# The thin last column block of A in two graph products: one fetch into one buffer in place of two fetches into two

## The chip, the cores and the metric

The kernel runs on one core of a Trainium2 chip. The metric is the device time of that core in microseconds (us); 904 us is about the time of one execution. An execution is one launch of the whole four-layer network. "PE" is the matrix engine, "DVE" the vector engine, "ACT" the scalar (activation) engine, "POOL" the general engine, "SP" the engine that here only issues transfers; "SPq" is its queue.

## The reference, cut to what matters

Four graph layers run one after the other on N = 2708 nodes with F = 128 features. `A` (`adj` in the code) is a dense stored 2708 x 2708 float32 matrix, 29.3 MB. Each layer ends in `x = layernorm(x + layer(x))`.

```python
# layer 0: x = LN(x + (D^-1/2 (A+I) D^-1/2 @ x) @ W.T + b)
# layer 1, attention:
XW  = x @ W
den = exp(leaky_relu(s_row[:, None] + s_col[None, :]))
num = A @ den
att = where(num != 0, den / num, 0)
H   = A @ (att @ XW)                 # product "a1" of the kernel
x   = LN(x + H)
# layer 2, hyperbolic:
xt  = logmap0(proj(mobius_add(proj(mobius_matvec(W2, x)), bias)))
s   = A @ xt                         # product "a2"
x   = LN(x + proj(expmap0(relu(logmap0(proj(expmap0(s)))))))
# layer 3:
out = concat((A > 0) @ x, (A < 0) @ x) @ Wn + bn * diag(A) + (A @ x) @ We + be * diag(A) + x
x   = LN(x + out)                    # products "a3": A and the mask of A
```

## The kernel before, in words

Features lie on the 128 partitions and nodes run along the free axis, so a product with A is computed transposed, from the stored `adjT`. The contraction over nodes is cut into NT = 22 row tiles of 128 (the last has 20 rows), and the result into NB = 6 column blocks: five of BW = 512 columns and a last one of 148. One block of one product is 22 accumulating matmuls of 128 x 128 against 128 x 512 (or 128 x 148) float32. A float32 matmul shows as two matmul passes in the trace, so a block has 44 passes and a whole product 264.

The stage before (the attention) ends at about 474 us. After it the function `fast_rest` runs the products a1, a2 and a3 one behind the other, and streams A from DRAM once for each. `pieces(b, i)` fetches half a column block: 11 row tiles of block `b` (KH = 11), with `i` the half. The second half has ten full row tiles by one transfer and the 20-row tile by another. A wide half is 2,816 KB or 2,560 + 40 KB; a half of the thin block is 814 KB or 740 + 11.6 KB. Each call takes the next of three buffers in turn: two in the pool `cb_a` and one in `cb_b`, by `n % 3`, where `n` counts the calls. All three have the shape of a wide half. A buffer is free again when the last matmul (in a3 also the last mask) that reads the piece in it is done. All the transfers stand in SP's queue in the order of the calls, and SP waits at each one for its buffer. In the kernel before, a1 takes pieces 0 to 11, a2 takes 12 to 23 and a3 takes 24 to 35. I call them by these numbers where needed, or by product, block and half: "a2 block 0, first half".

`product(weights, b, name, upto)` issues the matmuls of one block, up to row tile `upto`, and asks for a piece when it reaches the first tile of a half. `after_attention(b)` works on a finished block of a1: residual, layer norm, and the first product of layer 2 (`mx`). `hyperbolic(q, ta, tb)` does the scalar work of layer 2 on groups of row tiles, (0, 12) after block 2, (12, 20) after block 4 and (20, 22) after block 5, in long chains of tiny vector instructions with square roots, logarithms and tanh on ACT between; it ends by writing `h` (`q_b` in the trace), the weights of a2, one row tile after the other (line 1717). `meanwhile` puts the first six matmuls of a2's block 0, two at a time, between the steps of block 5 of `after_attention`, with a hand-written order on PE.

`after_hyperbolic(b)` works on a finished block of a2: sums (`su`), a mean that is spread back (`mean`), a factor that is spread back (`pg`), a norm (`st`, `pr_l`), and the products `pp` that make `edge` and `node`, the weights of a3. In a3 each row tile takes one float32 matmul from the piece itself (line 1867) and two one-pass matmuls (line 1876) against a mask of the piece that DVE makes (line 1855), in tiles of at most six row tiles; two such mask tiles exist.

Two seams matter in what follows: the one from a1 to a2, and the one from a2 to a3. At each of them the thin block 5 of one product is followed by the wide block 0 of the next. Apart from the hand-written stretch, a scheduler sets the order of the instructions on each engine from its own expectation of when the operands are ready[...].

Of the kernel before, what the change touches and what calls it, by code (L numbers as in the profile page):

```python
# [10 lines left out]
F32 = mybir.dt.float32  # L11
# [10 lines left out]
P = 128  # L22
NT = (N + P - 1) // P
NP = NT * P
BW = 512
NB = (N + BW - 1) // BW
KH = NT // 2
# [17 lines left out]
def rows(t):  # L45
    return min(P, N - t * P)


def width(b):
    return min(BW, N - b * BW)  # L50
# [7 lines left out]
def kernel(  # L58
# [130 lines left out]
    @contextmanager  # L189
    def queued(*engines):  # L190

        traced = nc.cur_bb.bb.instructions
        n = len(traced)
        with ExitStack() as st:
            for e in engines:
                if e in latest:
                    st.enter_context(tc.issue_after(latest[e]))
            yield
        for i in traced[n:]:
            if i.engine in engines:  # L200
                latest[i.engine] = i
# [5 lines left out]
    def bslice(b):  # L207
        return slice(b * BW, b * BW + width(b))
# [632 lines left out]
    with tc.tile_pool(name="tri", bufs=1) as tp:  # L841
# [241 lines left out]
        for c in range(NB):  # L1083
            w = width(c)
# [83 lines left out]
    with ctx_keep:  # L1168
# [11 lines left out]
        with tc.tile_pool(name="sort", bufs=1) as st_p:  # L1180
# [45 lines left out]
            for b in range(NB):  # L1226
                w, cs = width(b), bslice(b)
# [174 lines left out]
    def grouped_attention(u_sb, rows_g):  # L1402
        adj_h = adjT.rearrange("k (h w) -> (k h) w", h=2)
        chunks = [(0, BW), (BW, 2 * BW), (2 * BW, HALF)]
        with tc.tile_pool(name="main", bufs=1) as mp:
# [146 lines left out]
            for t in range(HALF // P, NT):  # L1552
                node_major_u(t, t % 2)

    def fast_rest(u_sb, pieces, scratch_pool, blk):


# [17 lines left out]
        def product(weights, b, name, upto=NT, fixed=False):  # L1575


            w = width(b)
            if name not in begun:
                begun[name] = [psum.tile([P, BW], F32, tag=f"acc{3 + b % 3}", name=name), 0, None]  # L1580
            acc, done, pc = begun[name]
            for k in range(done, upto):
                i, t = divmod(k, KH)
                if t == 0:
                    pc = pieces(b, i)
                kw = rows(k)
                with queued(PE) if fixed else nullcontext():
                    nc.tensor.matmul(  # L1588
                        acc[:, :w],
                        lhsT=weights[:kw, k, :],  # L1590
                        rhs=pc[:kw, t, :w],
                        start=(k == 0),
                        stop=(k == NT - 1),
                    )
            begun[name] = [acc, upto, pc]
            return acc

        def meanwhile(b, n):

            if b == NB - 1:  # L1600
                product(h, 0, "a2_0", n, True)
                return queued(PE)
            return nullcontext()
# [178 lines left out]
        for b in range(NB):  # L1782
            after_attention(b, product(u_sb, b, f"a1_{b}"))
            if b in spans:
                hyperbolic(b, *spans[b])
# [53 lines left out]
        for b in range(NB):  # L1839
            after_hyperbolic(b, product(h, b, f"a2_{b}"))  # L1840
# [5 lines left out]
        for b in range(NB):  # L1846
            w, cs = width(b), bslice(b)
            acc = psum.tile([P, BW], F32, tag=f"acc{3 + b % 3}", name=f"a3_{b}")
            for i in range(2):
                pc = pieces(b, i, i == 1)  # L1850
                for ma, mb in ((0, 6), (6, KH)):
                    mask = scratch_pool.tile([P, 6, BW], F32R, tag="mask", name=f"mask{b}_{i}_{ma}", bufs=2)
# [10 lines left out]
                    for t in range(ma, mb):  # L1863
                        k = i * KH + t
# [28 lines left out]
    with tc.tile_pool(name="cb_b", bufs=1) as cb_b, tc.tile_pool(name="cb_a", bufs=2) as cb_a:  # L1893
        u_sb = xw
        rows_g = cb_b.tile([P, KH, BW], F32, tag="cb", name="rows_g").rearrange("p t c -> p (t c)")
        grouped_attention(u_sb, rows_g)
        with (
            tc.tile_pool(name="rest", bufs=1) as rest_p,
            tc.tile_pool(name="blk2", bufs=2) as blk2,
        ):  # L1900
            pools["blk"] = blk2
            count = {"n": 0}

            def pieces(b, i, diagonal=False):

                n = count["n"]
                count["n"] += 1
                pool = cb_b if n % 3 == 2 else cb_a
                t = pool.tile([P, KH, BW], F32, tag="cb", name=f"cb{n}")
                w, cs = width(b), bslice(b)  # L1910
                full = KH - i
                k0 = i * KH * P
                if n < 3:

                    with tc.issue_after(marks["begun"]):
                        nc.gpsimd.memset(t[:, :, 0:1], 0.0)
                nc.sync.dma_start(
                    out=t[:, :full, :w],
                    in_=adjT[k0 : k0 + full * P, cs].rearrange("(t p) c -> p t c", p=P),
                )  # L1920
                if i:
                    kw = rows(NT - 1)
                    nc.sync.dma_start(out=t[:kw, full, :w], in_=adjT[k0 + full * P :, cs])
                    if diagonal:
                        nc.sync.dma_start(
                            out=t[kw : kw + 1, full, :w], in_=diag_d[cs, :].rearrange("c o -> o c")
                        )
                return t

            fast_rest(u_sb, pieces, rest_p, blk2)  # L1930
# [47 lines left out]
```

## Time and profile before

Three runs took 903.33, 903.94 and 903.99 us.

| what | value |
|---|---|
| median of the runs | 903.94 us |
| the profiled execution: its span | 903.4 us |
| PE busy | 847.1 us, 94% of the span |
| DVE / ACT / POOL busy | 554.8 / 389.0 / 206.1 us |
| mean granted PE clock | 0.973 of full speed |
| HBM read | 179.33 MB, 203 GB/s over the span |
| first and last matmul of a1 | 474.1 and 586.6 us |
| first and last matmul of a2 | 589.7 and 717.1 us |
| first and last matmul of line 1867 (a3) | 720.8 and 894.1 us |
| the chain that ended last | 84% PE, 8% DMA, 5% DVE, 2% ACT |

In the profile's lists of work in order of time, a line gives the start and the length in us, the engine, the source line, the operation with its operands and shape, and the count of the instructions merged into it. A bracket says how long the engine had sat idle before the line, and what ended the wait. The granted clock tells what share of its full rate the matrix engine was given in a stretch.

### The profile page before, as it was taken

What the parts mean: (1) busy time and instruction counts of PE and PEld (TensorE: products, weight loads), DVE (VectorE), ACT (ScalarE), POOL (GpSimd) and SP (SyncE); (2) the same over time, 40 slices, a digit from 0 to 9 for tenths busy, and PEclk for the clock granted to TensorE, in tenths of its full rate; (3) what the DMA queues carried; (4) which work ended last, traced back from release to release, by engine and by line L of the source; (5) the groups of instructions that cost most, each with busy time, mean ns of one, the idle gap of its engine ahead of it and who ended that gap; (6) DMA issues with size and microseconds to landing.
All of it is one profiled execution on the core that took longest, in us unless ns stands there. A gap on an engine that the chain in (4) does not pass through costs nothing.

```text
span 903.4 us, 9470 instructions
## 1 busy us (share of the span) xinstructions
PE 847.1 (94%) x3268; PEld 429.5 (48%) x3268; DVE 554.8 (61%) x1189; ACT 389.0 (43%) x681; POOL 206.1 (23%) x176
## 2 busy tenths in 40 slices
PE   3699999699899999999999999989999899999996
PEld 3244454335344445444454444534444555555555
DVE  4777548988788888889971226375644564233313
ACT  3776433215787777787761115273332221000000
POOL 5221000101788885776500000000000000000000
PEclk9799999989899999999999999999999999999997
DMA  9995684596596555445534776496764565474410
GB/s 341 366 361 204 120 245 144 182 383 215 180 372 213 151 162 158 142 153 154 154 122 168 266 268 229 134 335 238 265 222 132 210 211 198 145 253 142 160 42 19
DMA packets 95979, 184.30 MB, mean 204 GB/s; under 512 B 6446, under 2 KB 23551, under 8 KB 95668
## 3 DMA queue, kind: packets, MB, share of 16 engines
q1 hardware_dynamic: 85700, 143.82, 46.2%
q0 software_dynamic: 8352, 37.76, 13.0%
q10 hardware_dynamic: 1872, 2.04, 0.7%
q8 instruction: 28, 0.46, 0.2%
q14 instruction: 27, 0.22, 0.1%
HBM read 179.33 MB, written 4.28 MB: 203 GB/s over the span
## 4 chain that ended last, share of the span: by engine, by line
PE 84%; DMA 8%; DVE 5%; ACT 2%; issue 1%; SPq 0%; DVEq 0%; ACTq 0%
PE a L1588 22%; PE num L1464 13%; PE uacc L1491 13%; PE a L1867 12%; PE a L866 10%; PE a L1876 6%; DMA A<-in_adjT_dram 4%; DMA B<-in_adjT_dram 3%; PE t L803 1%; DMA cb<-in_adjT_dram 1%; PE pp L1825 1%; DVE counts L1051 1%; PE mx L1695 1%; PE su L251 0%; DVE work L267 0%
## 5 line engine op out<-in xcount | busy, mean ns | idle before, releaser
L1415 POOL DMA_INDIRECT rows_g<-in_adjT_dram,row_i x52 | 131.2, 2523 | 90.6 <-PE num L1464 40.9
L1469 ACT ACTIVATE ln<-num,inval,occ_l 128x512 f32<-128x512 f32 x156 | 107.5, 725 | 52.7 <-DVE rows_g L1467 48.7
L1867 PE MATMUL a<-cb,ut 128*128 128x512 f32 (+2 forms) x264 | 125.8, 559 | 1.3 <-DMA cb<-in_adjT_dram 1.3
L1491 PE MATMUL uacc<-att,xw_g 128*128 128x512 f32 (+1 forms) x312 | 126.3, 542 | 0.0
L1876 PE MATMUL a<-mask,node 128*128 128x512 f32 (+2 forms) x264 | 120.3, 537 | 0.7 <-DVE mask L1855 0.7
L1464 PE MATMUL num<-rows_g,w_all 128*128 128x512 f32 (+1 forms) x276 | 113.6, 544 | 0.8 <-ACT ln L1469 0.8
L1588 PE MATMUL a<-cb,q_b 128*128 128x512 f32 (+2 forms) x264 | 111.7, 561 | 1.8 <-DMA cb<-in_adjT_dram 1.8
L866 PE MATMUL a<-A,q_b 128*128 128x512 f32 (+2 forms) x264 | 106.1, 549 | 1.5 <-DMA A<-in_adjT_dram 1.5
L1588 PE MATMUL a<-cb,xw 128*128 128x512 f32 (+2 forms) x264 | 107.3, 550 | 0.0
L1467 DVE COPY rows_g<-num 2x512 f32<-2x512 f32 x150 | 88.0, 612 | 15.8 <-PE num L1464 14.6
L1491 PEld LDWEIGHTS uacc<-att,xw_g 128*128 128x128 f32 x312 | 59.1, 190 | 59.1 <-issue 50.0
L1483 DVE TENSOR_TENSOR att<-att,ln 128x1354 f32<-128x1354 f32 x52 | 80.5, 1548 | 2.0 <-ACT ln L1479 2.0
L1464 PEld LDWEIGHTS num<-rows_g,w_all 128*128 128x128 f32 x276 | 49.8, 190 | 53.8 <-issue 39.6
L1876 PEld LDWEIGHTS a<-mask,node 128*128 128x128 f32 (+1 forms) x264 | 48.5, 193 | 49.4 <-issue 47.6
L230 ACT ACTIVATE sq_l<-s 128x512 f32<-128x512 f32 (+1 forms) x11 | 6.6, 604 | 148.4 <-DVE s L1885 116.7
L1479 ACT ACTIVATE ln<-ln 128x1354 f32<-128x1354 f32 x52 | 69.3, 1333 | 1.7
L1855 DVE TENSOR_SCALAR mask<-cb 128x3072 fp32r<-128x3072 f32 (+5 forms) x24 | 33.5, 1395 | 59.3 <-PE a L1876 58.6
L866 PEld LDWEIGHTS a<-A,q_b 128*128 128x128 f32 (+1 forms) x264 | 45.9, 191 | 50.0 <-issue 46.7
L1588 PEld LDWEIGHTS a<-cb,q_b 128*128 128x128 f32 (+1 forms) x264 | 45.1, 192 | 46.9 <-issue 42.8
L1588 PEld LDWEIGHTS a<-cb,xw 128*128 128x128 f32 (+1 forms) x264 | 45.1, 190 | 46.5 <-issue 46.5
L1074 ACT ACTIVATE xw<-A 128x2048 f32<-128x2048 f32 (+3 forms) x36 | 57.0, 1582 | 8.3 <-DMA b_s<-in_b_dram 4.4
L1456 DVE TENSOR_SCALAR att<-q_b,gj_l 128x1354 f32<-128x1354 f32 x52 | 48.2, 927 | 12.6 <-PE uacc L1491 12.5
(445 smaller groups left out, 899.5 us busy)
## 6 DMA issues: line engine op xcount, KB each, us to landing
cb<-in_adjT_dram SPq DMA_DIRECT2D x15, 2816.0 KB
cb<-in_adjT_dram SPq DMA_DIRECT2D x15, 2560.0 KB
A<-in_adjT_dram SPq DMA_DIRECT2D x25, 1024.0 KB
B<-in_adjT_dram SPq DMA_DIRECT2D x18, 1024.0 KB
cb<-in_adjT_dram SPq DMA_DIRECT2D x3, 814.0 KB
cb<-in_adjT_dram SPq DMA_DIRECT2D x3, 740.0 KB
ut<-in_adjT_dram SPq DMA_DIRECT2D x2, 1024.0 KB
A<-in_adjT_dram SPq DMA_DIRECT2D x5, 296.0 KB
```

The costliest lines, as they stand in the source:

```text
L866: nc.tensor.matmul(acc[c][:, :w], lhsT=z[:kw, k, :], rhs=t[:kw, i, :w], start=c not in begun, stop=(d == NB - 1 and k == NT - 1), skip_gro ...
L1074: checks[d, c] = nc.scalar.activation(below[:, :nt, :w], t[:, :nt, :w], AF.Relu, scale=-1.0, accum_out=neg_sum[:, NB * c + d : NB * c + d ...
L1415: got = nc.gpsimd.indirect_dma_start(out=gat[q], out_offset=None, in_=adj_h, in_offset=bass.IndirectOffsetOnAxis(ap=row_i[:, h, g : g + 1] ...
L1464: nc.tensor.matmul(num[:, : cb - ca], lhsT=w, rhs=gat[q][:, ca:cb], start=True, stop=True)
L1467: nc.vector.tensor_copy(gat[q + 1][0:2, ca:cb], num[0:2, : cb - ca])
L1469: nc.scalar.activation(ln_n[q][:, ca:cb], num[:, : cb - ca], AF.Ln, scale=occ_l[:, g : g + 1], bias=inval[:, g : g + 1],)
L1479: nc.scalar.activation(ln_n[q], ln_n[q], AF.Exp, scale=-1.0)
L1483: nc.vector.tensor_mul(att[q], att[q], ln_n[q])
L1491: nc.tensor.matmul(uacc[h][c][:, : cb - ca], lhsT=xw_g[:, g, :], rhs=att[q][:, ca:cb], start=(g == 0), stop=(g == GM - 1),)
L1588: nc.tensor.matmul(acc[:, :w], lhsT=weights[:kw, k, :], rhs=pc[:kw, t, :w], start=(k == 0), stop=(k == NT - 1),)
L1867: nc.tensor.matmul(acc[:, :w], lhsT=edge[:ke, k, :], rhs=pc[:ke, t, :w], start=(k == 0), stop=False, skip_group_check=True,)
L1876: nc.tensor.matmul(acc[:, :w], lhsT=node[:kw, k, j, :], rhs=mask[:kw, t - ma, :w], start=False, stop=(k == NT - 1 and j == 1), skip_group_ ...
```

## The change

`product` asks for the thin block (b = 5) as one piece of all 22 row tiles, and `pieces` gives it one buffer of the tile's real width, 22 x 148 elements a partition, 13,024 bytes, where a wide half is 11 x 512, 22,528 bytes. The 21 full row tiles come by one transfer of 1,554 KB and the 20-row tile by a second of 11.6 KB. This holds for a1 and a2. a3 still asks for two halves of its thin block. With it the calls of `pieces` are numbered anew: a1 takes pieces 0 to 10, a2 takes 11 to 21 and a3 takes 22 to 33; the rule `n % 3` is unchanged.

```diff
             acc, done, pc = begun[name]
+            half = NT if b == NB - 1 else KH
             for k in range(done, upto):
-                i, t = divmod(k, KH)
+                i, t = divmod(k, half)
                 if t == 0:
-                    pc = pieces(b, i)
+                    pc = pieces(b, i, n_full=half)
...
-            def pieces(b, i, diagonal=False):
+            def pieces(b, i, diagonal=False, n_full=KH):
...
                 pool = cb_b if n % 3 == 2 else cb_a
-                t = pool.tile([P, KH, BW], F32, tag="cb", name=f"cb{n}")
                 w, cs = width(b), bslice(b)
-                full = KH - i
+                cols = BW if n_full == KH else w
+                t = pool.tile([P, n_full, cols], F32, tag="cb", name=f"cb{n}")
+                ends = i == 1 or n_full == NT
+                full = n_full - ends
                 k0 = i * KH * P
...
-                if i:
+                if ends:
                     kw = rows(NT - 1)
                     nc.sync.dma_start(out=t[:kw, full, :w], in_=adjT[k0 + full * P :, cs])
```

## The prediction

> **What bounds the kernel now.** I read the shares of busy time first: PE is busy 94% of the span, so only stretches in which PE is idle, or runs slowly, can give time back. In the groups of instructions, the two float32 groups of the last three products that wait at all wait for a fetch of A:
>
> ```profile
> L1867 PE MATMUL a<-cb,ut 128*128 128x512 f32 (+2 forms) x264 | 125.8, 559 | 1.3 <-DMA cb<-in_adjT_dram 1.3
> L1588 PE MATMUL a<-cb,q_b 128*128 128x512 f32 (+2 forms) x264 | 111.7, 561 | 1.8 <-DMA cb<-in_adjT_dram 1.8
> ```
>
> By that view the stake is 3.1 us. It is more, as PE's work in order of time shows at the seam from a1 to a2:
>
> ```profile
> 586.77 1.16 PE L1695 MATMUL mx<-w2ext,x 128*128 128x129 f32 x8
> 589.69 1.98 PE L1588 MATMUL a<-cb,q_b 128*128 128x512 f32 x4 [1.76 <-DMA cb<-in_adjT_dram]
> 591.51 0.50 PE L1612 MATMUL st<-mean_w,asq 128*128 128x1 f32 x4
> 591.88 1.96 PE L1588 MATMUL a<-cb,q_b 128*128 128x512 f32 x4
> 596.17 0.66 PE L244 MATMUL pr<-ident,rstd 128*128 128x128 f32 x2 [2.33 <-DVE t L1717]
> 596.62 3.29 PE L1588 MATMUL a<-cb,q_b 128*128 128x512 f32 x4
> 599.75 0.61 PE L1695 MATMUL mx<-w2ext,x 128*128 128x129 f32 x4
> ```
>
> See the bracket of the second line (the piece is late), the bracket before `pr` (a vector result is late), and that four passes take 3.29 us where four took 1.96. The same view at the seam from a2 to a3:
>
> ```profile
> 714.74 2.68 PE L1588 MATMUL a<-cb,q_b 128*128 128x148 f32 x18
> 719.05 0.40 PE L273 MATMUL pg<-two_pg,sel 128*128 128x128 bf16 x4 [1.64 <-DVE two_pg L267]
> 720.75 1.13 PE L1867 MATMUL a<-cb,ut 128*128 128x512 f32 x2 [1.30 <-DMA cb<-in_adjT_dram]
> 722.55 1.22 PE L1876 MATMUL a<-mask,node 128*128 128x512 f32 x2 [0.67 <-DVE mask L1855]
> 723.57 1.91 PE L1867 MATMUL a<-cb,ut 128*128 128x512 f32 x2
> ```
>
> Busy time and granted clock by stretches of 1 us tell the rest. Columns: stretch, length, busy time with counts of PE, PEld, DVE, ACT and POOL, the granted clock, the DMA share, GB/s.
>
> ```profile
> 597.00:598.00 1.00, 1.00 (x2) 0.34 (x1) 0.69 (x5) 0.43 (x2) 0.00 (x0) 0.50 1.05 389
> 600.00:601.00 1.00, 1.00 (x6) 0.57 (x5) 0.93 (x8) 0.58 (x2) 0.00 (x0) 1.00 1.05 383
> 724.00:725.00 1.00, 1.00 (x2) 0.00 (x0) 0.71 (x2) 0.98 (x2) 0.00 (x0) 0.50 1.06 391
> ```
>
> After each group of pauses the clock is halved, here for about 3.4 us. The issue queue says why the pieces are late. A row merges neighbours: the first is the issue at 558.54 and one that ends at 570.63.
>
> ```profile
> 558.54 12.09 SPq L1917 DMA_DIRECT2D cb<-in_adjT_dram  x2
> 579.89 4.11 SPq L1917 DMA_DIRECT2D cb<-in_adjT_dram  x2
> 587.51 17.53 SPq L1917 DMA_DIRECT2D cb<-in_adjT_dram  x2
> 697.39 0.58 SPq L1923 DMA_DIRECT2D cb<-in_adjT_dram  x1
> 709.58 4.99 SPq L1917 DMA_DIRECT2D cb<-in_adjT_dram  x2
> ```
>
> The thin halves hold two of three buffers, so a2's first half (piece 12) is issued at 579.89 and a3's (piece 24) at 709.58, some 8 us before PE needs them. Piece 24 is released to PE 11.1 us after issue, while the next pieces share the engines (385 to 412 GB/s).
>
> [...]here SP waits 187.7 us in all for matmuls of line 1588 ahead of line 1917.
>
> **The change part by part.** Sums are against the span of 903.4 us; the median is 903.94, 0.5 us above it, and I carry the difference over.
>
> *Buffers.* With the thin block in one buffer, a2's first half takes the buffer that block 4's first half leaves at 570.6, not 579.9. The nearest undisturbed estimate of its landing: DMA moves about 390 GB/s when full, 2,816 KB is 2.88 MB, 7.4 us;[...] 9.6 us. It lands at 580.2; PE needs it at 587.9. The second half follows at 579.9 (lands about 588.7) and block 1's first half still at 587.5 (about 596). At the other seam a3's first half is issued where 697.4 was, 12.2 us earlier relative to PE's work. Both fetch waits, 1.76 and 1.30 us, go, with 8 us of cover.
>
> *The thin fetch.* It is issued where its first half was (558.5) and needed at 581.9. The halves, in 592-byte runs, each kept the engines busy for 3 to 4 us; 1,554 KB is then 6 to 8 us[...]. It lands by 569, hidden by 12 us of block 4. In a2 the spare is the same. One issue fewer (0.37 us of SP) lies in SP's waiting: nothing.
>
> *The order at the first seam.* The built programs' orders differ. PE's is the same up to a2's row tile 11. On ACT the root of block 5's variance (line 1685) moves up, directly behind block 4's root, and needs no table load of its own (1.28 us before). On DVE its reciprocal (1686) moves from behind block 4's chain to its start. So after `mx` at 587.93: four passes to 589.7, `st` to 590.1, root to 590.5, reciprocal to 590.9, while PE works to 591.9. The 2.33 us wait goes. With both pauses gone the slow clock goes: from 596.17 to 600.19 PE did what takes 0.22 + 1.75 + 0.44 = 2.4 us at full clock, so 1.6 us. First seam: 1.76 + 2.33 + 1.6 = 5.7 us.
>
> *What is late next.* Row tiles 12 to 19 of `h` come from the chain of block 4. In the new order 22 instructions of block 5 stand among it, ahead of its last factor. Bounds: nothing, if they fall in the 0.2 us steps of the dependent chain, or 22 x 0.2 = 4.4 us. Eight of them pair with eight dependent steps and are free; 14 at 0.1 us, less some gaps, are about 1.1. Row tile 12 was written at 601.86 to 602.2; I take 603.3. PE's new order puts row tiles 6 to 11 and three matmuls of block 1 before it: 594.5 + 9 x 0.875 = 602.4. New wait 0.9 us; at the upper bound 4.2, and then a slow clock of 1.6 again. Row tiles 20 and 21 were ready at 616.5; their chain starts 5.7 us earlier and waits behind two table loads, so about 612.7 to 613, against PE at about 613.8: no wait.
>
> *The second seam.* PE now reaches a3's block 0 with its piece landed. DVE's first two masks (1.76 and 1.48 us) move ahead of block 4's sums, and ten of a3's matmuls (four float32, six mask) ahead of `pg`: 4 x 0.88 + 6 x 0.23 = 4.9 us of work. The masks push block 4's chain about 1.3 us, to `two_pg` at 720 where it was 719.0, in before's times; PE asks at 722.3. So 1.64, 1.30 and 0.67 us all go. From 722.55 to 726.47 PE did what takes 0.46 + 0.86 + 0.36 + 0.57 = 2.25 us: 1.6 us of slow clock. Together 5.2 us. Given back: DVE's third mask now stands before block 4's norm, waits for PE's sixth row tile, and takes 1.76; then 2.15 us to `two_pr_l`; PE has three row tiles, 4.0 us, to cover 3.9 plus hand-over. I take 0.3 us for this and the `pp` behind it; bounds 0 and 2.2, the cover less one row tile and the mask's wait doubled.
>
> Sum: 5.7 + 5.2 - 0.9 - 0.3 = 9.7 us. After the seams PE waited for nothing until the last norm, so a gain made here reaches the end. Span 893.7, median 894.2.
>
> **The rivals.**
> A: *the hyperbolic chain takes the place of the fetch.* For it: h's rows were only 3 us ahead of PE, and the chain gets 22 insertions. Against: most fit in gaps, and block 5's part starts earlier. If the upper bound holds, the first seam gives 5.7 - 5.8, nothing: 903.94 - 4.9 = 899.0.
> B: *the vector queue blocks at the second seam*: third mask, norm and `pp` each late, with a slow clock again. For it: the 0.1 us margin above. Against: each stall is short. It leaves the first seam's 4.8: 899.1.
> C: *no change.* Both A and B, or the pieces don't move: 903 to 904. Against: SP's queue is limited by nothing but the buffers.
> D: *slower.* The masks now stand ahead of block 4's sums[...]. If a3's first half lands late, because one thin fetch drains slowly ahead of it, every us beyond some 2.4 of cover stops DVE, then PE. It was to land in 9.6 us; to eat 9.7 us as well it must be 12 us late, so take 22 us. Just beyond, at 24 us: 906. The measured rates speak against it; a loss by something I don't see goes here too.
>
> **How the numbers follow.** Forecast 70%, A 12%, B 6%, C 5%, D 7%. The forecast's own range is 893 (no new wait: 903.94 - 10.9) to 897. I give 892.6 to 899.2, which takes in A and B and leaves out C and D. Differences under 0.2% (1.8 us) can't be told from none. Faster 0.70 + 0.12 + 0.06 = 0.88, same 0.05, slower 0.07.
>
> **What would show it.** No fetch bracket at lines 1588 and 1867 of the seams; no bracket at `pr` near 590 to 592; `pg` without a wait; the clock at 1.00 through both seams; a2's end at 717.1 less about 4.8. A bracket by DVE's line 1717 at a2's row tiles 12 to 20 over 1 us, or a second slow stretch, shows A; one at `pr_l` or `pp`, B. I am wrong if a fetch is still late, or if time goes in a stage that the change doesn't touch.

## The result, and the profile after

| | runs | median, us | lowest to highest |
|---|---|---|---|
| before, beside it | 4 | 903.63 | 899.73 to 903.99 |
| changed | 4 | 893.93 | 892.15 to 894.80 |

The ratio is 0.9895, with an interval of 0.9876 to 0.9913: faster by 9.7 us. A later set of five runs gave 893.42 and a ratio of 0.9889 (0.9868 to 0.9909).

The profiled execution of the changed kernel has a span of 890.3 us, 13.1 less than that of before. That is more than the runs gained, so I split it by stage, from PE's work in order of time. Each number is the start of a product's last matmul with A:

| | first of a1 | last of a1 | last of a2 | last of a3 (the float32 ones) |
|---|---|---|---|---|
| before | 474.1 | 586.6 | 717.1 | 894.1 |
| changed | 472.7 | 585.2 | 710.0 | 881.1 |

a1 starts 1.4 us earlier; over all profiled executions of this study it starts anywhere from 471.5 to 477.6, whatever the kernel. That is scatter of the stages before it, which the change doesn't touch. a1 itself takes 112.5 us in both. From a1's end to a2's end, the stretch with the first seam, it is 130.6 and 124.8, so 5.8 us gained; from a2's end to a3's end, with the second seam, 176.9 and 171.1, so 5.8 (taken before rounding to 0.1). These two stretches carry the rest of the document, since the scatter of a1's start is not in them.

The groups of instructions of the changed kernel, at the two groups that waited for a fetch before (busy us and mean ns of one, then the idle time ahead; the lines have moved by one):

```profile
L1868 PE MATMUL a<-cb,ut 128*128 128x512 f32 (+2 forms) x264 | 123.6, 550 | 0.0
L1589 PE MATMUL a<-cb,q_b 128*128 128x512 f32 (+2 forms) x264 | 110.4, 555 | 0.1
```

The idle time has gone from 1.3 and 1.8 us to 0.0 and 0.1. The mean matmul is shorter too (559 to 550 ns, 561 to 555): the stretches at half clock are gone. PE's work in order of time at the first seam:

```profile
585.38 1.16 PE L1696 MATMUL mx<-w2ext,x 128*128 128x129 f32 x8
586.38 1.88 PE L1589 MATMUL a<-cb,q_b 128*128 128x512 f32 x4
...
590.26 0.38 PE L244 MATMUL pr<-ident,rstd 128*128 128x128 f32 x2
590.48 1.88 PE L1589 MATMUL a<-cb,q_b 128*128 128x512 f32 x4
```

and at the second:

```profile
708.85 1.42 PE L1589 MATMUL a<-cb,q_b 128*128 128x148 f32 x8
710.19 1.13 PE L1868 MATMUL a<-cb,ut 128*128 128x512 f32 x2
...
715.14 0.39 PE L273 MATMUL pg<-two_pg,sel 128*128 128x128 bf16 x4
...
723.24 0.40 PE L273 MATMUL pr_l<-two_pr_l,sel 128*128 128x128 bf16 x4
```

No line has a bracket, which these lists put only at idle times over 0.15 us. Where `mx` ends, a2's first matmul begins, and where a2 ends, a3's first begins. The four passes behind `pr` take 1.88 us, where they took 3.29. The clock by stretches, at the places that were at 0.50 before or close behind them:

```profile
597.00:598.00 1.00, 1.00 (x4) 0.51 (x3) 1.00 (x13) 0.68 (x3) 0.00 (x0) 1.00 0.00 0
724.00:725.00 1.00, 1.00 (x5) 0.53 (x4) 0.36 (x1) 0.00 (x0) 0.00 (x0) 1.00 0.00 0
```

The clock, third from the end, is 1.00. The last two, DMA share and GB/s, are nothing: the fetch that ran at about 390 GB/s here in before is already over. SP's queue shows why:

```profile
557.15 0.37 SPq L1920 DMA_DIRECT2D cb<-in_adjT_dram  x1
...
568.87 10.00 SPq L1920 DMA_DIRECT2D cb<-in_adjT_dram  x2
...
689.82 12.97 SPq L1920 DMA_DIRECT2D cb<-in_adjT_dram  x2
```

557.15 is the thin block of a1 in one transfer. The issue at 568.87 is a2's first half (its second half closes the row, at 578.87), 17.5 us before PE uses it at 586.38; before, it was issued 9.8 us ahead. At 689.82 a3's first half is issued, 20.4 us before its use.

### The profile page after: what moved, and what is told of

The parts are those of the page before. It is cut to its first block, busy times and chain, and to the rows that moved or that the text cites. A ratio compares the mean times of both kernels' runs of the same rounds, so it can differ in the third digit from the quotient of the medians.

```text
span 890.3 us, 9463 instructions
## 1 busy us (share of the span) xinstructions
PE 840.4 (94%) x3268; PEld 425.4 (48%) x3268; DVE 552.1 (62%) x1189; ACT 386.2 (43%) x679; POOL 205.3 (23%) x176
## 4 chain that ended last, share of the span: by engine, by line
PE 85%; DMA 7%; DVE 5%; ACT 2%; issue 1%; SPq 0%; DVEq 0%; ACTq 0%
PE a L1589 22%; PE num L1464 13%; PE uacc L1491 13%; PE a L1868 11%; PE a L866 10%; PE a L1877 6%; DMA A<-in_adjT_dram 4%; DMA B<-in_adjT_dram 3%; PE t L803 1%; PE pp L1826 1%; DVE counts L1051 1%; PE su L251 1%; PE mx L1696 1%; DVE work L267 0%; PE st_l L251 0%
## 5 line engine op out<-in xcount | busy, mean ns | idle before, releaser
L1868 PE MATMUL a<-cb,ut 128*128 128x512 f32 (+2 forms) x264 | 123.6, 550 | 0.0
```

What stands on the lines that cost most here:

```text
L1868: nc.tensor.matmul(acc[:, :w], lhsT=edge[:ke, k, :], rhs=pc[:ke, t, :w], start=(k == 0), stop=False, skip_group_check=True,)
```

## The experiments

All numbers of a stretch are from the profiled execution of that kernel. "First seam" is the stretch from a1's end to a2's end, "second seam" from a2's end to a3's end.

| kernel | median, us | ratio to before, interval | first seam | second seam |
|---|---|---|---|---|
| before | 903.6 to 904.3 | | 130.6 | 176.9 |
| changed | 893.93 | 0.9895 (0.9876 to 0.9913) | 124.8 | 171.1 |
| again | 893.42 | 0.9889 (0.9868 to 0.9909) | 124.8 | 171.7 |
| only_a1 | 899.09 | 0.9951 (0.9932 to 0.9969) | 124.8 | 175.7 |
| only_a2 | 897.26 | 0.9934 (0.9914 to 0.9955) | 128.9 | 171.1 |
| two_buffers | 903.68 | 1.0003 (0.9986 to 1.0020) | 130.5 | 176.7 |
| two_transfers | 894.97 | 0.9906 (0.9881 to 0.9931) | 124.8 | 171.1 |
| root_early | 905.28 | 1.0012 (0.9999 to 1.0025) | 130.1 | 176.9 |
| root_late | 899.44 | 0.9953 (0.9929 to 0.9977) | 130.8 | 171.2 |
| filled | 902.92 | 0.9993 (0.9981 to 1.0004) | 128.9 | 176.8 |

**again.** The changed kernel once more.

> The changed kernel once more, for a tight figure against the kernel before on the same chip. Both seams together gained 5.8 and 5.9 us in the profiled executions (11.7 in all), while the medians differ by 9.7. If the seams are the whole of it, the difference of the medians here is 10 to 12 us and the rest of the 9.7 was scatter between runs; if some of the 11.7 is given back elsewhere, it stays below 10.

The ratio held, and the medians differ by 10.6 us, inside the 10 to 12 expected if the seams are the whole of it. The second seam was 171.7 instead of 171.1: in this execution the thin last block of a3 ran 3.4 us at half clock, as it did in before, and in the profile of the changed kernel it did not. Up to the start of that thin block the second seam is 163.68 us in before, and 158.45 and 158.44 in the two executions of the change. So 5.2 of the 5.8 us belong to the change, and 0.6 is a clock that happened to stay up. It is only 0.6 because at full clock PE then waits 0.89 us for `pr_l` in that block (at 873.20); at half clock, in `again`, that wait doesn't occur.

**only_a1, only_a2.** The thin block in one buffer in one product only.

```diff
-            half = NT if b == NB - 1 else KH
+            half = NT if b == NB - 1 and name[:2] == "a1" else KH
```

The other one has "a2" there.

> The thin block as one piece in a1 alone. If the two seams are independent, it gains the first seam's 5.7 us (5 to 6.5), and the trace shows the pauses and the half clock of before still at the seam from a2 to a3. Rival: the gain hangs on both changes (a start of a2 that is earlier is only waited off at the next seam), then it gains under 2 us.

> The thin block as one piece in a2 alone. Independent seams: it gains the second seam's 5 to 6.5 us, with the first seam as before (1.76 us of fetch wait, 2.3 us before pr, half clock). With the run of a1 alone it adds up to the whole change within 1 us. Rival as there: under 2 us.

The stretches come apart as the theory has it: only_a1 has the whole gain of the first seam (124.8), only_a2 the whole gain of the second (171.1). The ratios multiply to 0.9885, against 0.9889 for the whole. The medians are looser: 5.0 and 6.8 us under before, where 5 to 6.5 was expected of each, and 11.7 together against 10.6 for `again`. Each kernel also has a little in the seam that its edit leaves alone. In only_a1 it is 1.2 us: the third pause of the second seam, 0.67 us for a mask, didn't occur (the clock was at 0.50 earlier there, from 715.63 to 719.04, and a3's first two passes took 1.83 us where before took 1.13), and the thin last block stayed at full clock (0.6). In only_a2 it is 1.6 us, and PE's work in order of time shows how:

```profile
587.30 3.51 PE L1589 MATMUL a<-cb,q_b 128*128 128x512 f32 x4 [1.94 <-DMA cb<-in_adjT_dram]
...
593.59 0.40 PE L244 MATMUL pr<-ident,rstd 128*128 128x128 f32 x2 [0.61 <-DVE t L1718]
```

The clock was at 0.50 right behind the first pause, from 587.00 to 590.41, so four passes took 3.51 us there; PE came to `pr` that much later, and waited 0.61 us for the root instead of 2.33. A slow clock ahead of a wait cost nothing here; behind the last wait, as in before, it cost about 1.6 us.

**two_buffers, two_transfers.** Which part of "one piece" counts, the buffer or the transfer? In two_buffers the 21 full row tiles come as in the change, in one transfer of 1,554 KB, but the 20-row tile goes to the next buffer in turn, so that two buffers are held as before. In two_transfers there is one buffer, and the 21 row tiles come in two transfers, as the halves did. In two_buffers

```diff
+                end = t
+                if n_full == NT:
+                    n = count["n"]
+                    count["n"] += 1
+                    pool = cb_b if n % 3 == 2 else cb_a
+                    end = pool.tile([P, n_full, cols], F32, tag="cb", name=f"cb{n}")
...
-                    nc.sync.dma_start(out=t[:kw, full, :w], in_=adjT[k0 + full * P :, cs])
+                    nc.sync.dma_start(out=end[:kw, full, :w], in_=adjT[k0 + full * P :, cs])
```

and in two_transfers

```diff
+                cuts = (0, KH, full) if n_full == NT else (0, full)
+                for ca, cb in zip(cuts, cuts[1:]):
+                    nc.sync.dma_start(
+                        out=t[:, ca:cb, :w],
+                        in_=adjT[k0 + ca * P : k0 + cb * P, cs].rearrange("(t p) c -> p t c", p=P),
+                    )
```

> The thin block by one transfer for its 21 full row tiles, as in the change, but the 20-row tile goes into the next buffer, so that the block again holds two of the three until its last matmul. Theory (the buffer is what matters): a2's and a3's first halves are issued as late as before, both fetch waits and both slow clocks are back, and the time is that of the kernel before within 1.5 us. Rival (the one large transfer, its fewer issues, is what matters): the time is that of the changed kernel, about 10 us faster.

> The change, with the 21 full row tiles of the thin block fetched by two transfers (11 and 10 row tiles) into the one buffer. Theory: same as the changed kernel within 1 us (about 10 us under the kernel before), since the buffers are the same and the issue costs 0.4 us of SP's waiting. Rival (the single transfer matters): slower than the changed kernel by over 2 us.

With two buffers held, nothing is left of the gain (1.0003), and both pauses of the first seam stand as they did:

```profile
587.62 1.98 PE L1589 MATMUL a<-cb,q_b 128*128 128x512 f32 x4 [1.72 <-DMA cb<-in_adjT_dram]
...
594.13 0.66 PE L244 MATMUL pr<-ident,rstd 128*128 128x128 f32 x2 [2.36 <-DVE t L1718]
```

With one buffer and two transfers all of it is there (0.9906, stretches equal to the change's). It is the buffer. How the bytes are cut makes no difference that these runs can tell.

**root_early, root_late.** In the first seam the change does two things: the piece comes early, and the scheduler moves the root of block 5's variance ahead of block 4's chain. root_early is before, with its late piece, but with the new place of the root: block 4's hyperbolic group is issued behind block 5's part of `after_attention`, and its first logarithm is held behind block 5's reciprocal. root_late is the change, with its early piece, but with block 5's root held behind block 4's tanh, as it was.

Root_early, against before:

```diff
+            marks["root"] = nc.vector.reciprocal(rstd[:, ta:tb], rstd[:, ta:tb]).ins
...
+            with tc.issue_after(marks["root"]):
+                arg = atanh(f"a{q}", z, n)
...
-            if b in spans:
+            if b == 2:
...
+        for b in (4, 5):
+            hyperbolic(b, *spans[b])
```

Root_late, against the change:

```diff
+            with tc.issue_after(marks["tanh"]) if b == NB - 1 else nullcontext():
+                nc.scalar.activation(rstd[:, ta:tb], st[:, :n], AF.Sqrt, bias=eps_c)
...
+            marks["tanh"] = nc.scalar.activation(rn, arg, AF.Tanh).ins
```

> The kernel before, with its two pieces in two buffers, but block 5's root of the variance on ACT and its reciprocal on DVE ahead of block 4's logarithm, as the changed kernel has them. Theory: the fetch is still late (1.76 us), the 2.33 us before pr go, but block 4's chain now waits for the late root by about 2 us, and PE at a2's row tile 12 waits for it 2 us: 901 to 903 in all, against 904.0 of before. Rival (at the first seam the order alone brings the gain, not the fetch): 898 to 899.5, as with the change in a1 alone.

> The changed kernel, but with block 5's root held behind block 4's tanh on ACT, as the kernel before had it. The fetches are as early as in the change. Theory: no fetch bracket, but PE stands before pr for about 4.5 us, and the clock halves after it (1.6 us): it loses 5 to 6.5 us against the changed kernel, so about 899. Rival (the early fetch alone is the gain of the first seam): within 2 us of the changed kernel.

Neither half brings more than 0.5 us in the first seam: 130.1 and 130.8 against 130.6, where both together give 124.8. With the root early and the piece late, `pr` doesn't wait any more, but block 4's chain now waits for block 5's reciprocal, that for the sum `st`, and that for PE, which stands at the late piece. The list of PE's waits, in the stretch from 585 to 640 us of root_early (total, times, longest), has what was saved at `pr` back at a2's later row tiles:

```profile
PE a L1588 <- DVE q_b L1717: 2.9, 2, 2.7
```

That made root_early a miss of my expectation on the slow side. With the piece early and the root late, PE gets to `pr` sooner and waits there for all of it:

```profile
595.45 0.40 PE L244 MATMUL pr<-ident,rstd 128*128 128x128 f32 x2 [4.36 <-DVE t L1719]
```

4.36 us is more than the two pauses of before together (1.76 + 2.33). The two waits were in a row; taking away one of them feeds the other. At the second seam the early piece and the new order were not taken apart in this way: only_a2 brings both, two_buffers takes both away.

**filled.** What is the half clock worth? Before, with added matmuls at PE's two pauses in the first seam, so that the engine works while it waits.

```diff
+        def fill(ps, n):
+            for _ in range(n):
+                nc.tensor.matmul(ps, lhsT=ident, rhs=x[:, :BW], start=True, stop=True)
...
+                    fill(st, 1)
...
+                    fill(pr, 2)
```

> The kernel before with three added matmuls (128x512 float32, into a scratch tile that is overwritten) in the first seam: one ahead of a2's first matmul, where the engine waits 1.76 us for the piece, two ahead of `pr`, where it waits 2.33 us. Buffers, fetches and the orders of DVE and ACT are those of before, so the piece and the root still come late, but the matrix engine is kept at work while it waits. The pauses should shrink to less than 1.2 us in all. Theory (the pauses halve the clock, and that costs about 1.6 us): no half clock in the first seam, a1's end to a2's end 128.9 where before has 130.5, second seam as in before, whole time about 902.4. Rival (what the half clock costs is taken from a wait that would be there anyway, or it is set by something else than the pauses): 130.5 and about 903.9.

PE's work in order of time, where the first and third lines are the added matmuls:

```profile
587.47 1.02 PE L1607 MATMUL st<-x,ident 128*128 128x512 f32 x2
589.48 1.98 PE L1588 MATMUL a<-cb,q_b 128*128 128x512 f32 x4 [0.98 <-DMA cb<-in_adjT_dram]
...
593.46 1.88 PE L1607 MATMUL pr<-x,ident 128*128 128x512 f32 x4
595.76 0.43 PE L244 MATMUL pr<-ident,rstd 128*128 128x128 f32 x2 [0.42 <-DVE t L1726]
```

The pauses shrank to 0.98 and 0.42 us, the clock stayed at 1.00 through the first seam, and the stretch is 128.9, or 1.7 us less: what the half clock cost here, about the 1.6 expected, can be had alone, by useless work. In the whole time it doesn't stand out (0.9993, interval up to 1.0004), since the scatter of the whole time is as large as it; I rest this on the stretch.

## Why the prediction was right

**The buffers: right.** a2's first half was to be issued when block 4's first half leaves its buffer, at 570.6 in before's times; it was issued at 568.87, which is 570.3 with the 1.4 us by which a1 ended earlier. a3's was to be issued where 697.4 was, which is 690.3 with the 7.1 us by which a2 ended earlier; it was at 689.82. Both fetch waits are gone. two_buffers shows that the buffer is the cause. The 9.6 us for a wide half to land held an estimate of 2.2 us beyond the transfer itself: in before a2's first half took 9.8 us from issue to release (579.89 to 589.69), 2.4 more than its 2.88 MB take at 390 GB/s.

**The thin fetch: right, with more room than forecast.** It was to keep the engines busy for 6 to 8 us. By the DMA view from 555 to 600 us they moved it from 558.4 to 564.0, 5.6 us, and stood idle from there to 569.6, when the next piece began.

**The order at the first seam: right.** Root at 590.5 and reciprocal at 590.9 in before's times were forecast; 588.83 and 589.13 were measured, which are 590.2 and 590.5 there. `pr` has no wait. root_late shows that without this step the seam gains nothing. ACT's work in order of time in before shows what the root stood behind there:

```profile
593.81 0.21 ACT L1736 ACTIVATE rn<-a4s 128x8 f32<-128x8 f32 x1 [0.81 <-DVE a4s L1734]
594.03 1.28 ACT L1685 ACT_TABLE_LOAD   x1
595.33 0.26 ACT L1685 ACTIVATE rstd<-st,eps_c 128x2 f32<-128x2 f32 x1
```

ACT sat idle for 0.81 us ahead of block 4's tanh, though PE had finished `st`, which the root behind it reads, at 592.01; the root ran at 595.33.

**Late next, the chain of block 4: the term that was mis-sized.** I put 0.9 us for a2's row tile 12, with bounds of 0 and 4.2. The wait is there, but it is about 0.3 us, too short for a bracket. PE's work in order of time:

```profile
592.64 7.89 PE L1589 MATMUL a<-cb,q_b 128*128 128x512 f32 x18
600.66 1.55 PE L1589 MATMUL a<-cb,q_b 128*128 128x512 f32 x3
```

The 18 passes of the first line start 0.43 us apart, so the next would have started at 600.37. Row tile 12 starts at 600.66, just behind its row of `h`, which was complete at 600.61. DVE's work in the changed kernel shows why the wait isn't longer:

```profile
597.11 0.17 DVE L1651 SCALAR_TENSOR_TENSOR b4s<-b4s,b4w 128x8 f32<-128x8 f32 x1
597.20 0.15 DVE L1651 SCALAR_TENSOR_TENSOR a5s<-a5s,a5w 128x2 f32<-128x2 f32 x1
597.31 0.17 DVE L1651 SCALAR_TENSOR_TENSOR b4s<-b4s,b4w 128x8 f32<-128x8 f32 x1
...
600.26 0.64 DVE L1718 SCALAR_TENSOR_TENSOR q_b<-q_b,ca,yt 128x128 f32<-128x128 f32 x2 [0.20 <-ACT yt L1779]
```

Block 5's steps (`a5s`) stand between block 4's (`b4s`), and block 4's still follow each other every 0.20 us, as in before, where eight of them in a row took 1.56. I had let eight of the 22 inserted instructions go free and charged 14 at 0.1 us, less some gaps. They cost nothing on balance: from the start of `mx` to the first of block 4's rows of `h` it took 14.88 us (585.38 to 600.26) where it had taken 15.09 (586.77 to 601.86). So for the chain the lower bound was the true value, and row tile 12 was complete at 602.0 in before's times, not 603.3. A wait is left because PE was early too: it would have started the row tile at 601.8 in before's times, not 602.4. Rows 20 and 21 were complete at 610.65 and 610.94, or 612.0 and 612.3 in before's times, against 612.7 to 613; no wait there, as forecast.

**The second seam: right, with the small loss that was charged.** `two_pg` was to come at 720 in before's times, 1.3 us later than it did, and PE to ask for `pg` at 722.3. The changed kernel's DVE has it complete at 713.10, or 720.2 in before's times, and PE asks at 715.14, or 722.2:

```profile
712.75 0.35 DVE L267 SCALAR_TENSOR_TENSOR two_pg<-term_pg,behind,rest_pg 128x128 bf16<-128x128 bf16 x1
...
719.27 1.76 DVE L1856 TENSOR_SCALAR mask<-cb 128x3072 fp32r<-128x3072 f32 x1 [1.02 <-PE a L1877]
...
722.83 0.35 DVE L267 SCALAR_TENSOR_TENSOR two_pr_l<-term_pr_l,behind,rest_pr_l 128x128 bf16<-128x128 bf16 x1
```

The last two lines are the thin spot. The third mask does stand ahead of block 4's norm and waits 1.02 us for PE; then `two_pr_l` is complete at 723.18, and PE starts `pr_l` at 723.24. These 0.06 us are no margin: in before, where PE stood waiting for `two_pg`, it started `pg` just as long behind the vector result (718.99 and 719.05). So PE waited here too, too briefly for a bracket. The second mask pass of the row tile ahead of `pr_l` starts at 722.82; elsewhere in this block the next pass starts 0.23 us behind such a pass, here 0.42. That is about 0.2 us lost, where I had worked out a margin of 0.1 and charged 0.3 for its loss.

**The clock: the size right, the reason not shown.** 1.6 us at a seam was forecast, and filled shows 1.7 at the first; at the second it was not measured alone. Which pauses bring the half clock was not shown; see the last section.

**The sum.** 5.8 and 5.2 us are 11.0 against a forecast of 9.7. Of the two terms given back, 0.9 and 0.3, about 0.3 and 0.2 came. And the pauses were longer than the brackets that I had added up. From the start of `mx` to a2's first pass it takes 2.92 us in before and 1.00 in the changed kernel; from the start of the second four passes (591.88, and 588.46 in the changed kernel) to `pr` it takes 4.29 and 1.80. So the two pauses of the first seam cost 1.92 and 2.49 us, where the brackets say 1.76 and 2.33: a bracket counts from the end shown for the pass before, and in an unbroken stream a pass is shown 0.59 us long, though the next starts after 0.43. The two sets of whole runs gained 9.7 and 10.6. That the first is just the forecast is partly luck: a gain of 11.0 lies within the scatter of these runs.

**The rivals.** A and B came about in the change only on a small scale, as waits of 0.3 and 0.2 us without a slow clock. A's mechanism is real, though: root_early shows it at 2.7 us, and it takes a late piece for that. D's long stall of DVE didn't occur, since both masks found their piece landed.

## What to carry to other kernels

Where a ring of buffers feeds a bound engine, look for a small piece that takes a full slot: giving it one slot in place of two buys lead time for the next large piece without a byte more of memory. Before pricing one wait, look for the next one on the same engine and for what feeds it: here an earlier fetch alone, and an earlier root alone, were worth next to nothing (0.5 us at most), and both were worth 5.8 us. Compare stretches between two fixed events of the trace when a change is about as small as the scatter of the whole time.

## What the runs showed of the hardware

In the profile of before the clock falls at 596.03 and 722.32, at the two seams, and at 882.75, in the thin last block of a3, and comes back 3.41 us later each time. In filled it stayed at 0.50 for twice as long at the second seam, from 718.79 to 725.62. Where the clock fell at the seams, PE had not stood idle for all of the 3.41 us before: it had been busy for 0.11 (root_late, up to 595.81) to 0.52 (only_a2, up to 587.00) of them. The 3.41 us ahead of the first fall in before, and those behind it:

```profile
592.62:596.03 3.41, 1.22 (x3) 0.19 (x1) 2.94 (x23) 2.14 (x4) 0.00 (x0) 1.00 1.05 386
596.03:599.44 3.41, 3.27 (x6) 1.75 (x7) 2.64 (x21) 1.70 (x3) 0.00 (x0) 0.50 1.05 375
```

PE was busy for 1.22 us, and the clock then was 0.50. The same for only_a2, ahead of its fall:

```profile
583.59:587.00 3.41, 1.77 (x12) 1.27 (x11) 0.81 (x5) 2.21 (x11) 0.00 (x0) 1.00 1.05 387
```

and a stretch of root_early with about as much work, 1.81 us:

```profile
605.97:609.39 3.42, 1.81 (x4) 0.68 (x4) 1.99 (x17) 2.63 (x6) 0.00 (x0) 1.00 1.04 384
```

Here the clock stayed at 1.00, up to 612.83. So the length of a wait did not decide it: with 1.94 us in only_a2 the clock fell, with the longer 2.7 us in root_early it did not. Nor did the work in the stretch before by itself. In the stages before a1, 1.75 us of work in 3.41 (before, from 230.81) was followed by full clock and 1.97 in 3.42 (the changed kernel, from 219.09) by 0.50; in the thin last block of a3, 3.01 us in 3.41 (before, from 879.34) was followed by 0.50 and 3.02 in 3.42 (the changed kernel, from 867.62) by full clock. What sets the clock is open: the pauses as its cause were my reading of before, borne out only as far as filled, with shorter pauses, kept 1.00 through the first seam. About 1.6 us at a seam, the estimate from before's passes, can come or go with it.
